# Convolution operand from a transposed input, row statistics on ScalarE, and the gate ahead of its neighbours

## The chip, the cores and the metric

The kernel runs on one core of one Trainium2 chip. The metric is the device time of one launch in microseconds, from the first instruction to the last. The engines are named as in the profile: PE is TensorE's matmul, PEld its weight load, DVE is VectorE, ACT is ScalarE, POOL is GpSimd, and SP is SyncE, which here issues nearly all DMAs as one queue.

## The reference, cut to what matters

The input x has 4 batches of 1024 rows of 2048 values. Each row is normalized and modulated, convolved along its 2048 values with a kernel K that comes from a state-space model, gated and added to x. Then each row is normalized and modulated again and goes through a 2048 by 2048 weight with a low-rank update, and is gated and added again.

```python
mod = (_silu(L0_c) @ L0_wmod).reshape(L0_c.shape[0], 6, 1, -1)
sa, ca, ga, sb, cb, gb = (mod[:, i] for i in range(6))
ga = (2 * (ga >= 0) - 1) * jnp.maximum(jnp.abs(ga), 0.25)    # gb likewise
h = _layernorm(x, axis=-1) * (1 + ca) + sa
K = _s4_kernel(...)                                          # 2048 taps
y = irfft(rfft(h, n=2*L) * rfft(K, n=2*L))[..., :L]          # causal convolution
x = x + ga * (y + D[0] * h)
h = _layernorm(x, axis=-1) * (1 + cb) + sb
x = x + gb * (h @ W.T + bias + low_rank_update(h))
```

All arithmetic of the matmuls is done in pairs of float16 numbers, a high and a low part, with three products for each.

## The kernel before, in words

**Tiles.** A "row" in this text is a block of 128 input rows, r = 0 to 31, so that a row tile is 128 x 2048 in float32 (1 MB). Eight rows are one batch. A chunk is 128 of the 2048 values, so that a row has 16 chunks.

**Modulation.** `section` multiplies the conditioning vector with one sixth of `wmod`: 16 loads `wm` of 1 MB (`mod_load`) and as many groups of four small matmuls `modps` (`mod_mm`, L317). A section becomes columns (`mod_column`: `sa`, `ca`, `sb`, `cb`) or a gate (`mod_gate`, L342 to L347). Sections 1, 0 and 2 are done first, since the convolution needs them; sections 4, 3 and 5 come later as filler.

**The convolution kernel.** `s4` works out K; its last steps are 32 tiny matmuls `s4rp` (L175) and `s4kp`. `toeplitz` writes K to DRAM and reads it back as a 128 x 2048 tile `kb` whose row p is shifted by p, so that slices of it are Toeplitz blocks. [...] a matmul with the reversed identity `rev` (L263) turns the rows round. Then `kb` is split into six float16 tiles `kh0`, `kl0` and so on, for the even blocks, the odd minus even, and the shifted difference (L281 to L285).

**One row.** `conv_load` fetches x. `stats` takes mean and variance with four `bn_stats` (L540) and `bn_aggr` on DVE, and `rstd` (L69 to L73) the inverse deviation. `conv_prep` makes the operand: `normalize` writes `n` on DVE (L557), then for each quarter (four chunks) PE transposes four 128 x 128 blocks into PSUM (`tp`, L578), ACT takes them out with scale and shift (`t`, L582; L587 for rows 0 and 1), DVE adds pairs of chunks (`sm`, L590), and ACT and DVE split `t` and `sm` into high and low parts (`hc`, `hs`, L592 and L593). `conv_mm` runs 108 matmuls (L614) in six families, `ya`, `yb`, `ya` for each half of the row; a copy `qs` on ACT (L627) and four or five DVE operations (L631 to L641) turn the sums into the new x, with its row sum. `conv_post` stores it in DRAM (`x1d`) and takes the second statistics with a squaring pass on ACT (L660), which writes its unused result over x.

**Early rows.** Rows 0 and 1 start before the shift `sa` and the gate are known (`EARLY = 2`). The shift's share is convolved by itself (`shift_conv`, L397) and added later (`shift_add`, L414), and the gate is applied in `conv_late`. `pace` places one `wm` step of sections 0 and 2 after every 2700 columns of convolution. For row 2, `behind` lets PE run `GCOL = 11000` columns ahead of the matmuls `gps` (L674), which spread the first gate over all partitions.

**Order.** The program text sets the order, row by row. Each row calls `tick` ten times, and `PLAN` says by letters what is put in at each call: `N` a quarter of the next operand, `T` the statistics of row r + 2, `F` the start of its operand, `P` the previous row's `conv_post`, `S` a step of the filler, `L` a step of the feed-forward's left operand in the last rows. The filler (`rest`) merges the low-rank update into the weight (`merge`: `lps`, `we`, `wch`, written to `wcd`) and does sections 4, 3 and 5. There are nine `S` per row from row 5 on, fewer before. The tile framework then places the instructions on the engines' queues and sets the waits.

```python
PLAN = ("PNSL", "NL", "NSL", "NTL", "SL", "SL", "SL", "SL", "FSL", "SSL")
WM, WMS = 3, 3
```

**Feed-forward.** After row 31, `ffn_unit` runs 5376 matmuls (L750) in seven products per unit. The left operand of later units (`left`, L700 to L713) is made beside it in its first half.

Of the kernel before, what the change touches and what calls it, by code (L numbers as in the profile page):

```python
# [34 lines left out]
class Net:  # L35
# [40 lines left out]
    def s4(self, pool):  # L76
# [69 lines left out]
        rp = self.tps.tile([P, 16, 8], F32, tag="t", name="s4rp")  # L146
# [19 lines left out]
        for n, (cc, sc) in enumerate(cps):  # L166
            tt(wq[n], wr[n], wq[n], ADD)
            v.reciprocal(wq[n], wq[n])
            stt(wr[n], cc, nl[:, 0:1], wq[n], MUL, MUL)
            tt(wi[n], wi[n], wq[n], MUL)  # L170
            yield
            for c in range(w // P):
                out = rp.rearrange("p (h g) v -> p g h v", h=2)[:, 4 * n + c]
                for i, x in enumerate((wr[n], wi[n])):
                    nc.tensor.matmul(  # L175
                        out, x[:, ds(P * c, P)], cf[:, i],
                        start=(n, c, i) == (0, 0, 0), stop=(n, c, i) == (1, 3, 1), skip_group_check=True,
                    )
        r = T([P, 8, 16], "s4R")
        v.tensor_copy(r.rearrange("p v k -> p k v"), rp)  # L180
# [51 lines left out]

    def toeplitz(self, pool):
        nc, v = self.nc, self.nc.vector
        rev = pool.tile([P, P], F32, tag="rev", name="rev")
        nc.gpsimd.memset(rev, 0.0)
        nc.gpsimd.affine_select(
            out=rev, in_=rev, compare_op=ALU.not_equal, fill=1.0, base=1 - P, pattern=[[1, P]], channel_multiplier=1
        )
# [15 lines left out]

        kb = pool.tile([P, D], F32, tag="kb", name="kb")
        src = bass.AP(tensor=kd.tensor, offset=kd.offset + 1, ap=[[1, P], [1, D]])
        nc.gpsimd.dma_start(out=kb, in_=src)
        self.kb = kb
        yield  # L260
        for q in range(4):
            ps = self.acc.tile([P, 512], F32, tag="a", name="kbps")
            nc.tensor.matmul(ps, rev, kb[:, ds(512 * q, 512)], start=True, stop=True)  # L263
            (v.tensor_copy if q % 2 else nc.scalar.copy)(kb[:, ds(512 * q, 512)], ps)
# [5 lines left out]
        for f in (0, 2, 1):  # L270
            hi = self.kpool.tile([P, HC * P], F16, tag=f"kh{f}", name=f"kh{f}")
            lo = self.kpool.tile([P, HC * P], F16, tag=f"kl{f}", name=f"kl{f}")
            h3, l3 = (x.rearrange("p (m t) -> p m t", t=P) for x in (hi, lo))
            if f == 0:
                src = ev
            else:
                src = pool.tile([P, 2, 512], F32, tag="kdif", name="kdif")
                src = src.rearrange("p a (c t) -> p (a c) t", t=P)
                if f == 1:
                    v.tensor_scalar(src[:, 0:1], ev[:, 0:1], -1.0, None, MUL)  # L280
                    v.tensor_tensor(src[:, 1:], od[:, 0 : HC - 1], ev[:, 1:], SUB)  # L281
                else:
                    v.tensor_tensor(src, od, ev, SUB)
            v.tensor_copy(h3, src)  # L284
            v.tensor_tensor(l3, src, h3, SUB)  # L285
            self.kf[f] = hi, lo
# [51 lines left out]
    def mod_gate(self, pool, name, bias=None):  # L338
# [8 lines left out]
        v.scalar_tensor_tensor(g, g, 1.0, m, SUB, MUL)  # L347
# [62 lines left out]
    def shift_add(self, pool, ys):  # L410
        g = pool.tile([P, D], F32, tag="gat", name="gsb")
        self.nc.gpsimd.dma_start(out=g, in_=self.gsd.rearrange("c t -> (c t)").partition_broadcast(P))
        for y in ys:
            self.nc.vector.tensor_tensor(y, y, g, ADD)  # L414
# [121 lines left out]
    def stats(self, pl, x, tag):  # L536
        v = self.nc.vector
        st = pl["sm"].tile([P, 4, 6], F32, tag="st" + tag, name="st" + tag)
        for q in range(4):
            v.bn_stats(st[:, q], x[:, ds(512 * q, 512)])  # L540
        mv = pl["sm"].tile([P, 2], F32, tag="mv" + tag, name="mv" + tag)
        v.bn_aggr(mv, st)
        rs = pl["sm"].tile([P, 1], F32, tag="rs" + tag, name="rs" + tag)
        self.rstd(pl["sm"], mv[:, 1:2], rs, 1, "r" + tag)
        if tag in ACTNORM:
            mb = pl["sm"].tile([P, 1], F32, tag="mb" + tag, name="mb" + tag)
            v.scalar_tensor_tensor(mb, mv[:, 0:1], -1.0, rs, MUL, MUL)
            return mb, rs
        return mv, rs

    def normalize(self, pl, x, st, tag):
        n = pl["n"].tile([P, D], F32, tag="n", name="n" + tag)
        m, rs = st
        if tag in ACTNORM:
            self.nc.scalar.activation(n, x, AF.Identity, bias=m, scale=rs)
        else:
            self.nc.vector.tensor_scalar(n, x, m[:, 0:1], rs, SUB, MUL)  # L557
        return n
# [6 lines left out]
    def conv_prep(self, pl, r, x, st, out, shift=True):  # L565
        nc, v = self.nc, self.nc.vector
        b = r // 8
        n = self.normalize(pl, x, st, "1")
        yield

        hc = [pl["h"].tile([P, NC, P], F16, tag=f"hc{x}", name=f"hc{x}") for x in range(2)]
        hs = [pl["h"].tile([P, HC, P], F16, tag=f"hs{x}", name=f"hs{x}") for x in range(2)]
        out[r] = hc, hs
        for c0 in range(0, NC, 4):
            tp = self.tps.tile([P, 4, P], F32, tag="t", name="tp")
            t = pl["t"].tile([P, 4, P], F32, tag="t", name="t")
            for k in range(4):
                nc.tensor.transpose(tp[:, k], n[:, ds(P * (c0 + k), P)], self.ident)  # L578
            for k in range(4):
                c = c0 + k  # L580
                if shift:
                    nc.scalar.activation(  # L582
                        t[:, k], tp[:, k], AF.Identity,
                        bias=self.sa[:, c, b : b + 1], scale=self.ca[:, c, b : b + 1],
                    )
                else:
                    nc.scalar.activation(t[:, k], tp[:, k], AF.Copy, scale=self.cae[:, c : c + 1])  # L587
            tv = t.rearrange("p (i e) n -> p i e n", e=2)
            sm = pl["t"].tile([P, 2, P], F32, tag="sm", name="sm")
            v.tensor_tensor(sm, tv[:, :, 0, :], tv[:, :, 1, :], ADD)  # L590
            for (hi, lo), src, sl in ((hc, t, slice(c0, c0 + 4)), (hs, sm, slice(c0 // 2, c0 // 2 + 2))):
                nc.scalar.copy(hi[:, sl], src)  # L592
                v.tensor_tensor(lo[:, sl], src, hi[:, sl], SUB)  # L593
            yield

    def conv_mm(self, pl, hs, x, tick, early, pace):
        nc, v = self.nc, self.nc.vector
        hc, hs = hs
        y = pl["y"].tile([P, D], F32, tag="y", name="y")
# [54 lines left out]
    def conv_post(self, pl, r, x, y, sums):  # L654
# [5 lines left out]
        nc.scalar.activation(x, y, AF.Square, bias=mn, accum_out=sq)  # L660
# [147 lines left out]
ACTNORM = ""  # L808

MR = 2  # L810
ACC, TPS = 5, 2
PLAN = ("PNSL", "NL", "NSL", "NTL", "SL", "SL", "SL", "SL", "FSL", "SSL")
LPLAN = ("LL", "LL", "LL", "LL", "L", "0", "")
R0 = 5
WM, WMS = 3, 3
ROWC = 2700
GCOL = 11000
# [15 lines left out]
def net(ctx: ExitStack, tc: tile.TileContext, io):  # L833
# [52 lines left out]
    for name, bufs in (("h", 2), ("n", 1), ("t", 2), ("y", EARLY), ("g", 1)):  # L886
        pl[name] = pool(left, "p1" + name, bufs)
# [25 lines left out]
    for _ in section(1, (wms, wmp)):  # L913
# [3 lines left out]
        if n == X0:  # L917
            load(0)
# [248 lines left out]
```

## Time and profile before

| | us |
|---|---|
| median of 3 runs | 2144.08 |
| lowest and highest run | 2141.26, 2145.41 |
| the profiled execution | 2141.87 |
| its span | 2140.1 |
| PE busy in it | 2082.4 (97%) |
| DVE busy | 1308.4 (61%) |
| ACT busy | 923.7 (43%) |
| first and last convolution matmul (L614) | 68.5 and 918.9 |
| first feed-forward matmul (L750) | 918.9 |

The page gives for each engine its busy time in the span. A group row of the page names a source line, the engine, what is written and read, and how many there were; then the busy time of the group, the mean duration of one, and the idle time of the engine just before them with what ended it. Recorded durations of neighbours on one engine may overlap, so that the busy time of a group is less than number times mean. A windows row gives, for a stretch of the span, the busy time of each engine with the number of instructions, then PE's granted clock, the mean share of the DMA engines and the rate. The DMA share is 0.98 in the first 60 us, and 0.57 in the feed-forward part.

### The profile page before, as it was taken

What the parts mean: (1) busy time and instruction counts of PE and PEld (TensorE: products, weight loads), DVE (VectorE), ACT (ScalarE), POOL (GpSimd) and SP (SyncE); (2) the same over time, 40 slices, a digit from 0 to 9 for tenths busy, and PEclk for the clock granted to TensorE, in tenths of its full rate; (3) what the DMA queues carried; (4) which work ended last, traced back from release to release, by engine and by line L of the source; (5) the groups of instructions that cost most, each with busy time, mean ns of one, the idle gap of its engine ahead of it and who ended that gap; (6) DMA issues with size and microseconds to landing.
All of it is one profiled execution on the core that took longest, in us unless ns stands there. A gap on an engine that the chain in (4) does not pass through costs nothing.

```text
span 2140.1 us, 28438 instructions
## 1 busy us (share of the span) xinstructions
PE 2082.4 (97%) x11113; PEld 1026.1 (48%) x11113; DVE 1308.4 (61%) x2353; ACT 923.7 (43%) x1695; POOL 6.3 (0%) x18
## 2 busy tenths in 40 slices
PE   7898999999999999999999999999999999999998
PEld 2344455555555555554545545555444444444444
DVE  5439898898979999665565565575533323332323
ACT  1325876677767777745454555555200000000000
POOL 0000000000000000000000000000000000000000
PEclk7999999999999999999999999999999999999999
DMA  9977566787776554387564564564794645454542
GB/s 401 373 307 278 225 227 265 285 310 262 276 278 227 187 192 173 139 346 258 190 241 180 202 240 179 203 235 172 283 341 163 192 151 167 164 170 165 177 157 69
DMA packets 127236, 484.11 MB, mean 226 GB/s; under 512 B 13608, under 2 KB 13768, under 8 KB 95998
## 3 DMA queue, kind: packets, MB, share of 16 engines
q1 hardware_dynamic: 126192, 477.55, 61.4%
q10 hardware_dynamic: 526, 2.63, 0.4%
q8 instruction: 87, 1.43, 0.3%
q0 software_dynamic: 384, 2.11, 0.2%
q14 instruction: 47, 0.39, 0.0%
HBM read 326.94 MB, written 155.30 MB: 225 GB/s over the span
## 4 chain that ended last, share of the span: by engine, by line
PE 67%; DVE 18%; ACT 6%; DMA 5%; issue 2%; SPq 0%; ACTq 0%; POOL 0%; DVEq 0%; POOLq 0%
PE fZ L750 22%; PE fY L750 15%; PE fX L750 15%; PE ya L614 5%; PE yb L614 3%; PE tp L700 3%; DVE wch L514 2%; PE modps L317 2%; DVE st L540 2%; DVE hc L593 2%; DVE y L641 2%; ACT x L660 2%; DMA wcd<-wch 1%; ACT t L582 1%; PE lps L486 1%
## 5 line engine op out<-in xcount | busy, mean ns | idle before, releaser
L750 PEld LDWEIGHTS <-lf 128*128 128x128 f16 x5376 | 526.0, 98 | 620.9 <-issue 1.4
L750 PE MATMUL fZ<-w,lf 128*128 128x512 f16 x2304 | 513.6, 379 | 0.8 <-ACT p L758 0.8
L750 PE MATMUL fX<-w,lf 128*128 128x512 f16 x1536 | 342.8, 379 | 0.0
L750 PE MATMUL fY<-w,lf 128*128 128x512 f16 x1536 | 342.0, 379 | 0.0
L614 PEld LDWEIGHTS <-hc 128*128 128x128 f16 x2304 | 215.3, 98 | 204.6 <-issue 41.6
L768 DVE TENSOR_TENSOR xo<-xo,gb 128x512 f32<-128x512 f32 x128 | 87.8, 690 | 238.7 <-DMA xo<-x1d 227.2
L582 ACT ACTIVATE t<-tp,sa,ca 128x128 f32<-128x128 f32 x480 | 188.1, 471 | 21.6 <-PE tp L578 12.9
L614 PE MATMUL ya<-kh,hs 128*128 128x512 f16 (+3 forms) x768 | 193.7, 326 | 3.7 <-DVE kh L284 2.6
L614 PE MATMUL ya<-kh,hc 128*128 128x512 f16 (+3 forms) x768 | 192.7, 328 | 3.8 <-ACT qs L627 3.6
L614 PE MATMUL yb<-kh,hc 128*128 128x512 f16 (+3 forms) x768 | 192.2, 327 | 1.8 <-DVE y L640 1.4
L758 ACT COPY p<-fZ 128x512 f32<-128x512 f32 x64 | 37.2, 581 | 286.8 <-PE fZ L750 272.1
L614 PEld LDWEIGHTS <-hs 128*128 128x128 f16 x1152 | 105.9, 98 | 108.6 <-issue 28.4
L758 ACT COPY p<-fX 128x512 f32<-128x512 f32 x32 | 18.7, 585 | 316.3 <-PE fX L750 210.4
L702 ACT ACTIVATE gt<-tp,sb,cb 128x256 f32<-128x256 f32 x256 | 124.9, 576 | 60.8 <-PE tp L700 60.8
L317 PE MATMUL modps<-wm,sct 128*32 128x512 f32 x768 | 118.8, 662 | 14.1 <-DMA wm<-in_wmod 14.1
L614 PE MATMUL ya<-kl,hc 128*128 128x512 f16 (+3 forms) x384 | 125.8, 328 | 0.0
L614 PE MATMUL ya<-kl,hs 128*128 128x512 f16 (+3 forms) x384 | 125.1, 326 | 0.7 <-DVE kl L285 0.7
L614 PE MATMUL yb<-kl,hc 128*128 128x512 f16 (+3 forms) x384 | 125.6, 327 | 0.0
L773 DVE TENSOR_TENSOR fin<-fX,gb 128x512 f32<-128x512 f32 x32 | 22.1, 692 | 128.4 <-PE fX L750 128.3
L593 DVE TENSOR_TENSOR hc<-t,hc 128x512 f16<-128x512 f32 x128 | 87.5, 684 | 6.6 <-ACT hc L592 6.4
L486 PE MATMUL lps<-lbh,lac 128*128 128x512 f16 x256 | 86.3, 379 | 1.2 <-DVE we L488 1.2
L578 PE MATMUL tp<-ident,n 128*128 128x128 f32 x512 | 79.3, 280 | 8.1 <-ACT t L582 6.3
(264 smaller groups left out, 2228.0 us busy)
## 6 DMA issues: line engine op xcount, KB each, us to landing
wm<-in_wmod SPq DMA_DIRECT2D x96, 1024.0 KB
lfd<-lf SPq DMA_DIRECT2D x112, 512.0 KB
lf<-lfd SPq DMA_DIRECT2D x112, 512.0 KB
x<-in_x SPq DMA_DIRECT2D x32, 1024.0 KB
x1d<-y SPq DMA_DIRECT2D x32, 1024.0 KB
x<-x1d SPq DMA_DIRECT2D x32, 1024.0 KB
xo<-x1d SPq DMA_DIRECT2D x128, 256.0 KB
out<-xo SPq DMA_DIRECT2D x128, 256.0 KB
```

The lines of the kernel that those rows point to most:

```text
L317: self.last = self.nc.tensor.matmul(self.modps[32 * g : 32 * g + 32, :], self.sct[:, j].rearrange("p r b -> p (r b)"), w[:, ds(512 * g, 512)],
L486: nc.tensor.matmul(ps, la[:, x, k, h], y[:, k, osl], start=(n == 0), stop=(n == 5))
L514: v.tensor_tensor(hl[:, :, 1, :], tv, hl[:, :, 0, :], SUB)
L578: nc.tensor.transpose(tp[:, k], n[:, ds(P * (c0 + k), P)], self.ident)
L582: nc.scalar.activation(t[:, k], tp[:, k], AF.Identity, bias=self.sa[:, c, b : b + 1], scale=self.ca[:, c, b : b + 1],)
L593: v.tensor_tensor(lo[:, sl], src, hi[:, sl], SUB)
L614: nc.tensor.matmul(pf[:, o:512], h, self.kf[f][z][:, ds(k0, 512 - o)], start=first, stop=(i == last and (x, z) == (1, 0)), skip_group_chec ...
L700: nc.tensor.transpose(tp[:, c, r], xs[r][:, ds(P * (c0 + c), P)], self.ident)
L702: nc.scalar.activation(t[:, c0 + c], tp[:, c], AF.Identity, bias=self.sb[:, c0 + c, b : b + 1], scale=self.cb[:, c0 + c, b : b + 1],)
L750: nc.tensor.matmul(ps[name], lf[i][:, k, x, :], wc[i][k // 4][:, k % 4, y, :], start=(first and n == 0), stop=(n == 3 * HC - 1), skip_grou ...
L758: nc.scalar.copy(t, ps[name])
L768: v.tensor_tensor(x, x, self.gbias[:, h], ADD)
```

## The change

It has five parts.

1. **The operand comes transposed.** The host lays x out a second time as `xT`, with the chunk's values on the partitions and the rows along the free dimension, for pairs of rows (a group g is rows 2g and 2g + 1). A quarter `xq` (four chunks of both rows, 0.5 MB) is loaded by `quarter_load`, five buffers in all. `quarter_norm` adds minus the mean and multiplies with the inverse deviation, which now vary along the free dimension, in two `tensor_tensor` passes over the quarter. `quarter_mod` applies scale and shift in place on ACT, for both rows at once. `split` makes `hc` and `hs`, with `hs` in halves instead of quarters. The 512 transposes `tp`, their evacuation and the tile `n` are gone.
2. **Statistics on ACT.** `stats` sums the row with one ACT pass, scales the sum on DVE, squares and sums in a second ACT pass, and takes `rstd`. The passes write to an unused tile `junk`. `spread` transposes the two 128 x 1 results, broadcast to 128 columns, with four PE transposes for each group into the PSUM tile `mrb`, where every partition then has all means and deviations. Statistics are made for row r + 3, and x is loaded for row r + 3. x is still loaded in the old layout, for the statistics and for the final sum.
3. **Opposite chunk rows.** In `xT`, and in the first two sections of `wmod`, the 128 values of a chunk stand in opposite order. The reversal of `kb` by matmul is gone; `kb` is loaded in two halves and split half by half. In `s4`, the 32 tiny matmuls become four of 16 x 512 and eight small transposes.
4. **Gate first.** The first gate tile and its `gps` matmuls come right after section 2 and before the other work of that place, and `shift_add` is held behind the gate's DVE chain (`issue_after(k.gated.ins)`). `GCOL` is 30000, and row 2 has its own tile `y2`, so that it needn't wait for those of rows 0 and 1.
5. **Plan and buffers.** `PLAN` differs for even and odd rows: `B` and `A` split a quarter for the next row, `X` loads a quarter, `K` spreads, `G` normalizes and modulates a quarter. There are eight `S` per row. `WM` is 2.

The diff, cut to its core:

```diff
+        sp = self.acc.tile([16, w], F32, tag="a", name="s4sp")
+        for i, x in enumerate((wr[n], wi[n])):
+            nc.tensor.matmul(sp, cf[:, i].rearrange("p h v -> p (h v)"), x, start=(i == 0), stop=(i == 1))
...
-        for q in range(4):
-            ps = self.acc.tile([P, 512], F32, tag="a", name="kbps")
-            nc.tensor.matmul(ps, rev, kb[:, ds(512 * q, 512)], start=True, stop=True)
-            (v.tensor_copy if q % 2 else nc.scalar.copy)(kb[:, ds(512 * q, 512)], ps)
...
+    def quarter_load(self, pl, g, q, blocks=(0, 1)):
+        t = pl["q"].tile([P, 2, 4, P], F32, tag="xq", name="xq")
+        b = slice(blocks[0], blocks[-1] + 1)
+        self.nc.sync.dma_start(out=t[:, b], in_=self.io["xT"][g, :, b, ds(4 * q, 4), :])
+        return t
+
+    def stats(self, pl, x):
+        nc, v = self.nc, self.nc.vector
+        st = pl["sm"].tile([P, 2], F32, tag="st", name="st")
+        nc.scalar.activation(self.junk, x, AF.Copy, accum_out=st[:, 0:1])
+        v.tensor_scalar(st[:, 0:1], st[:, 0:1], -1.0 / D, None, MUL)
+        sq = pl["sm"].tile([P, 1], F32, tag="sq1", name="sq1")
+        nc.scalar.activation(self.junk, x, AF.Square, bias=st[:, 0:1], accum_out=sq)
+        self.rstd(pl["sm"], sq, st[:, 1:2], 1, "r1", 1.0 / D)
+        return st
+
+    def spread(self, sts):
+        ps = self.tps.tile([P, 2, 2, P], F32, tag="t", name="mrb")
+        for b, st in enumerate(sts):
+            for i in range(2):
+                self.nc.tensor.transpose(ps[:, i, b], st[:, i : i + 1].to_broadcast([P, P]), self.ident)
+        return ps
+
+    def quarter_norm(self, t, ps, blocks=(0, 1)):
+        for i, op in enumerate((ADD, MUL)):
...
+            m = ps[:, i, b].unsqueeze(2).to_broadcast([P, n, 4, P])
+            self.nc.vector.tensor_tensor(t[:, b], t[:, b], m, op)
+
+    def quarter_mod(self, t, b, q, shift=True, blocks=(0, 1)):
...
+        for k in range(4):
+            c = 4 * q + k
+            x = t[:, bb, k]
...
+                self.nc.scalar.activation(
+                    x, x, AF.Identity, bias=self.sa[:, c, b : b + 1], scale=self.ca[:, c, b : b + 1]
+                )
+
+    def split(self, pl, h, t, q):
...
+        v.tensor_tensor(self.sm[:, ds(2 * (q % 2), 2)], tv[:, :, 0, :], tv[:, :, 1, :], ADD)
+        sl = slice(4 * q, 4 * q + 4)
+        nc.scalar.copy(hc[0][:, sl], t)
+        v.tensor_tensor(hc[1][:, sl], t, hc[0][:, sl], SUB)
+        if q % 2:
+            sl = slice(2 * q - 2, 2 * q + 2)
+            nc.scalar.copy(hs[0][:, sl], self.sm)
+            v.tensor_tensor(hs[1][:, sl], self.sm, hs[0][:, sl], SUB)
...
-PLAN = ("PNSL", "NL", "NSL", "NTL", "SL", "SL", "SL", "SL", "FSL", "SSL")
+PLAN = (
+    ("PBX", "BXL", "BXSL", "TSL", "BXSL", "SL", "KGSL", "SL", "GSL", "SL"),
+    ("PG", "GAL", "ASL", "TSL", "ASL", "SL", "ASL", "SL", "SL", "SL"),
+)
-WM, WMS = 3, 3
+WM, WMS = 2, 3
-GCOL = 11000
+GCOL = 30000
+QS = 5
...
+    k.gat = k.gate_tile(pl["g"], 0)
     take(nxt, 40)
-    k.shift_add(pl["g"], [ys[r][0] for r in range(2)])
+    with tc.issue_after(k.gated.ins):
+        k.shift_add(wms, [ys[r][0] for r in range(2)])
+    y2 = stp.tile([P, D], F32, tag="kb", name="y2")
```

## The prediction

> **What bounds the kernel now.** I read the page's busy line first, then the windows by stage, then the costliest groups, the waits and a piece of the timeline.
>
> ```profile
> PE 2082.4 (97%) x11113; PEld 1026.1 (48%) x11113; DVE 1308.4 (61%) x2353; ACT 923.7 (43%) x1695; POOL 6.3 (0%) x18
> ```
>
> TensorE (PE) is busy 97% of the whole span, but an average hides the stages. The windows (columns: window, length, busy us of PE, PEld, DVE, ACT, POOL, then granted clock, DMA share, GB/s) cut the span into start, the two early rows, the gate, rows 5 to about 25 with the weight merge beside them, the last rows, and the feed-forward part:
>
> ```profile
> 0.00:60.00 60.00, 41.47 (x185) 15.36 (x186) 34.01 (x127) 7.93 (x16) 3.92 (x13) 0.78 0.98 403
> 60.00:160.00 100.00, 93.84 (x583) 38.21 (x581) 40.17 (x83) 29.33 (x80) 1.51 (x3) 0.94 0.85 336
> 160.00:243.00 83.00, 69.97 (x400) 35.44 (x401) 72.97 (x168) 55.25 (x114) 0.51 (x1) 0.92 0.73 271
> 243.00:800.00 557.00, 545.95 (x3352) 288.35 (x3350) 503.48 (x1042) 396.63 (x802) 0.41 (x1) 1.00 0.67 248
> 800.00:919.00 119.00, 117.23 (x744) 68.93 (x742) 97.58 (x212) 85.63 (x181) 0.00 (x0) 1.00 0.47 173
> 919.00:2140.00 1221.00, 1213.94 (x5858) 579.80 (x5855) 560.24 (x727) 348.91 (x505) 0.00 (x0) 1.00 0.57 201
> ```
>
> From 243 on PE is busy 98% or more. From 243 to 919, 676 us, it holds 663.2 us of work; VectorE (DVE) holds 601.1 (89%) and ScalarE (ACT) 482.3 (71%). So PE bounds the convolution rows, and DVE follows only 62 us behind: that is the number to keep in mind. After 919 the change touches nothing.
>
> The groups that the change removes or resizes (busy us, mean ns of one):
>
> ```profile
> L578 PE MATMUL tp<-ident,n 128*128 128x128 f32 x512 | 79.3, 280 | 8.1 <-ACT t L582 6.3
> L582 ACT ACTIVATE t<-tp,sa,ca 128x128 f32<-128x128 f32 x480 | 188.1, 471 | 21.6 <-PE tp L578 12.9
> L540 DVE BATCH_NORM_STATS2 st<-x 128x6 f32<-128x512 f32 x128 | 84.0, 682 | 0.8 <-DMA x<-in_x 0.6
> L557 DVE TENSOR_SCALAR n<-x,mv,rs 128x2048 f32<-128x2048 f32 x32 | 42.9, 1340 | 0.1
> L593 DVE TENSOR_TENSOR hs<-sm,hs 128x256 f16<-128x256 f32 x128 | 53.4, 418 | 0.4 <-ACT hs L592 0.2
> L641 DVE SCALAR_TENSOR_TENSOR y<-y,x 128x1024 f32<-128x1024 f32 x60 | 73.0, 1216 | 0.5
> ```
>
> The PE timeline shows that transposes stand in the convolution's way. Here four take about half a us between two matmuls of one family:
>
> ```profile
> 807.71 0.38 PE L614 MATMUL yb<-kl,hc 128*128 128x512 f16 x1
> 808.15 0.65 PE L578 MATMUL tp<-ident,n 128*128 128x128 f32 x4
> 808.64 0.59 PE L614 MATMUL yb<-kh,hc 128*128 128x512 f16 x2
> ```
>
> The waits show the early losses, and what DVE pays for a sum that ACT forms:
>
> ```profile
> PE gps L674 <- DVE mg L347: 9.9, 1, 9.9
> DVE r_v L69 <- ACT x L660: 17.1, 12, 2.2
> ```
>
> **What the Trainium skill says.** "TensorE: Matmul & The Clock Gate", Part 4 (PE-mode transpose), gives about 275 ns for a transpose inside a kernel. The trace agrees on the duration (280) and corrects the price: overlapped, one occupies PE for 79.3/512 = 0.155 us. "Perfetto Trace Analysis", Identifying the Most-Contended Engine, warns that matmul busy time does not show how near PE is to its limit. In 243 to 919 the 2919 conv matmuls take 504.1 us, 0.173 each; a 512-column one starts every 0.216 us in the timeline and a row averages 384 columns, so 0.162 is their floor. The busy share is nearly real. "VectorE: DVE Perf Modes", The TRN2 errata, prices a float32 tensor_tensor at (N+151)/0.96 ns: 1224 for 1024 elements, and the tier table keeps it at one element per cycle, PSUM operand or not. The trace has 1216 to 1219 for 1024 elements, and 683 for 512 with PSUM (y<-ya,gat). "ScalarE: Activation LUTs", Rules for kernel authors, has about 0.3 us plus 0.83 ns per element, 0.51 for 256: an estimate, on the high side, since the 512-wide cast measures 0.640 where it gives 0.72.
>
> **The change, part by part, 243 to 919.** Here 26 rows are prepared (416 transposes); 24 rows get statistics.
>
> PE: 416 transposes go, 51.4 + 12.3 = 63.7 us in the windows of that tile. The spread adds 4 transposes for each pair of rows: 13 x 4 x 0.155 = 8.1. PE falls from 663.2 to 607.6.
>
> DVE: 96 bn_stats go (0.656 each, 63.0), 24 aggregates (0.26, 6.2), 26 normalizations (1.34, 34.8). In place of the last come 8 tensor_tensor of 1024 elements per pair, reading mean and scale from PSUM: 13 x 8 x 1.22 = 126.9. This is the dear part: one two-scalar pass becomes two full passes. The hs subtraction, 104 of 0.417, becomes 52 of 0.684: -7.8. One small scaling per row: 24 x 0.15 = 3.6. Sum +18.7: DVE rises from 601.1 to 620.
>
> ACT: 416 evacuations go (163.0). In comes the modulation from SBUF, 208 of 128x256, at 0.425 (cast of that size) to 0.51 (the page): 88 to 106; two passes over each row, 24 x 2 x (2.00 + 0.19) = 105; hs casts -11. Sum about +28: 510 us.
>
> So **DVE, at 620, passes PE at 608**. The merge steps are dealt out 8 per row instead of 9, so that they end two rows or so later and the load is more even. When DVE set the pace before (180 to 220), it was busy 39.3 of 40 us. But now it stands behind ACT twice a row for a sum, so I take 96.5%: 642 us, a gain of 34. At 98% it is 633 (gain 43), at 92% 674 (gain 2).
>
> DMA: x is now fetched twice, 1 MB more per row in 2 KB pieces. At 248 GB/s and a share of 0.67, full use is about 370 GB/s; 27 MB more cost some 73 us of that and lift the share to about 0.82. SP is one queue: load x(r+3) waits for the previous row's last DVE pass and the xq loads for the split that frees a buffer, with mod and merge transfers behind them. Mod loads have two buffers instead of three; PE did not wait for them after 243, so I cost that at nothing. If their lead is gone, a wait costs up to the 7.9 us of the worst one in the start.
>
> **Before 243.** The reversal matmuls (5.4 us) go and kb comes in two halves. But DVE now has k's splitting (8.3 us by its rows) and eight norm passes (9.8) in line before row 0: from kb at about 55, plus 2.9 for the first splits, the first conv matmul comes at about 76, not 68.5. Eight quarters of xT, 4.2 MB at 400 GB/s, add 10 us of transfers ahead of the gate. Against that, 96 transposes (15.6 us) leave PE. At the gate, the 7 us of shift, statistics and normalization ahead of it on DVE step behind, and PE may run 30000 columns of row 2 instead of 11000 before it needs the gate: 19000 x 0.42 ns = 8 us of cover for the 9.9 us wait. DVE then has its backlog (early rows, 20 us), so row 4 starts about 8 us sooner. I take -8, bounds -20 and +8. The small s4 transposes replace tiny matmuls on an equal chain: nothing, within 1 us.
>
> Sum: profiled execution 2141.9 (span 2140.1), minus 34, minus 8 = 2100. The median shown is 2.2 above the profiled one: **2102**.
>
> **Rivals.** *PE stays the bound* (norm passes overlap better than I price them): 607.6 at the old 98.1% is 619, gain 57; with 15 early, 2072. For it: neighbouring DVE starts lie 0.60 apart where the record says 0.68. Against it: DVE would have to run at 99% or more.
>
> *ACT's sums become DVE's wait, and the kernel is slower.* The place is the pair L552 and L69 of the changed kernel: DVE scales the sum, ACT squares the row (2.2 us), DVE resumes. One or two DVE instructions stand between in the changed order, and at times none. Everything behind it in DVE's line, evacuation of y included, stands too, and PE at the spread. Before, the same handshake once a row cost 17.1 us over 32 rows; now there are two, and ACT is fuller. DVE at 97% is 639; it decides from (676 + 8 - 639)/26 = 1.7 us per row. At 2.5 us: 639 + 65 = 704, minus 8 early, 20 more than now: 2164.
>
> *The start eats it*: row 0 later by 15 rather than 7.5 and a stage at 94% (gain 16): about 2128.
>
> That the change doesn't do what it says is excluded for the transposes: its instruction order has 64 spread transposes instead of 512.
>
> **How the numbers follow.** DVE bound, near 2102 (2085 to 2120): 0.55. PE bound: 0.15. Start or utilization poor, 2120 to 2140: 0.14. No change, within 0.2% (4.3 us, about what a measurement can tell): 0.04. Slower: 0.12. So faster 0.84. The range 2068 to 2142 leaves about 0.05 below and 0.14 above.
>
> **What would show it.** Right: no tp group; transposes of mrb at about 10 us; norm passes at 1.2 us; in the conv rows DVE above 95% and PE below it; rows of about 25 us with merge (26.6 now); the feed-forward part at 1221 us. Wrong: DVE idle before L69 for more than 1.7 us per row, PE at 98%, or waits for xq or wm.

## The result, and the profile after

The changed kernel takes **2178.5 us** (median of 4 runs, 2171.4 to 2179.3) against 2143.5 for the kernel before on the same chip: a ratio of 1.0156, 95% interval 1.0133 to 1.018. The forecast was 2102, a gain of some 42 us, with 0.12 on slower. The prediction is wrong: the kernel is 35 us slower.

The profiled execution (2178.8 us, span 2177.0) splits as follows. "Row n's store" is the time at which SP issues the store of that row's result, read from SP's timeline. Here and below, the times of stages are those of one profiled execution of each kernel; the ratios of the experiments are to the kernel before on the same chip.

| | before | after | difference | forecast |
|---|---|---|---|---|
| row 0's store | 181.8 | 197.0 | +15.2 | |
| row 0's to row 4's store | 64.7 | 78.4 | +13.7 | both together: -8 |
| row 4's to row 31's store | 676.4 | 684.0 | +7.6 | -34 |
| last store to the end | 1217.2 | 1217.6 | +0.4 | 0 |

"The rows" below is the third line. Seven kernels that change only what lies before it, the changed kernel among them, gave 679.1 to 691.7, so differences under some 8 us there are not read as effects; the 7.6 themselves say no more than that the 34 did not come.

First the page's busy line after, which is no alarm in itself: PE went from 97% to 94%.

```profile
PE 2045.0 (94%) x10641; PEld 976.3 (45%) x10641; DVE 1324.4 (61%) x2263; ACT 990.5 (45%) x1503; POOL 6.4 (0%) x17
```

Then the windows after, by the same stages (length, busy us of PE, PEld, DVE, ACT, POOL, granted clock, DMA share, GB/s):

```profile
60.00:160.00 100.00, 76.37 (x435) 30.01 (x436) 47.70 (x100) 39.67 (x74) 1.30 (x3) 0.80 0.81 324
160.00:275.40 115.40, 94.76 (x532) 43.72 (x530) 72.58 (x149) 62.98 (x100) 0.98 (x2) 0.88 0.75 274
275.40:959.40 684.00, 629.78 (x3683) 317.62 (x3681) 615.63 (x1176) 525.78 (x811) 0.41 (x1) 0.98 0.75 270
959.40:2177.00 1217.60, 1211.41 (x5847) 578.91 (x5845) 556.90 (x723) 348.40 (x504) 0.00 (x0) 1.00 0.57 202
```

The third line is the heart of it. VectorE has 615.6 us of work in the rows, 4 from the 620 forecast, but it is busy 90.0% of the time, not 96.5%. PE is still the busiest, with 629.8 us or 92.1%; it is idle for 54 us and runs at a granted clock of 0.98. No engine is full. The same stretch of the kernel before (the last store comes at 922.9), where PE is idle for about 13:

```profile
246.50:923.00 676.50, 663.67 (x4085) 356.55 (x4084) 602.72 (x1252) 479.26 (x981) 0.41 (x1) 1.00 0.64 236
```

The groups of the rows, shapes kept apart (columns as before):

```profile
L571 DVE TENSOR_TENSOR xq<-xq,mrb 128x1024 f32<-128x1024 f32 x99 | 119.5, 1212 | 2.2 <-PE mrb L563 2.2
...
L579 ACT ACTIVATE xq<-xq,sa,ca 128x256 f32<-128x256 f32 x200 | 103.9, 588 | 28.3 <-DVE xq L571 28.3
...
L554 ACT ACTIVATE junk<-x,st 128x2048 bf16<-128x2048 f32 x24 | 48.0, 1999 | 4.3 <-DVE st L552 4.3
L551 ACT ACTIVATE junk<-x 128x2048 bf16<-128x2048 f32 x24 | 45.7, 1906 | 20.2 <-DMA x<-in_x 20.2
...
L563 PE MATMUL mrb<-ident,st 128*128 128x128 f32 x48 | 10.4, 289 | 6.9 <-DVE st L552 5.0 <-DVE st L73 1.8
```

The norm passes cost what was forecast (1.21). The modulation on ScalarE has a recorded duration of 0.588 each, but neighbouring records overlap: 200 of them keep ScalarE busy for 103.9 us, 0.52 each, at the upper end of the forecast's 0.425 to 0.51.

What PE waits for in the rows is scattered (columns: us in total, times, longest):

```profile
PE ya L625 <- DVE we L487: 9.4, 2, 6.8
PE ya L625 <- ACT qs L638: 8.9, 10, 3.2
PE mrb L563 <- DVE st L552: 5.0, 3, 1.9
PE lps L485 <- DVE y L651: 4.1, 2, 3.7
PE yb L625 <- DVE y L642: 4.0, 1, 4.0
```

Added up over all rows of this view, PE waits 53.8 us: 34.0 are ended by VectorE, 16.2 by ScalarE and 3.6 by a DMA. In the kernel before it is 12.0 (3.3, 8.7 and 0). Most of the places shown are evacuations of PSUM. Two moments show why they come late. On VectorE's timeline the sum y (L642), whose PSUM tile PE needs back, stands behind merge and norm passes of 1.2 us each; there is no gap between them:

```profile
802.93 1.22 DVE L513 TENSOR_TENSOR wch<-we,wch 128x1024 f16<-128x1024 f32 x1
804.07 1.22 DVE L571 TENSOR_TENSOR xq<-xq,mrb 128x1024 f32<-128x1024 f32 x1
805.20 1.22 DVE L530 TENSOR_TENSOR we<-we 128x1024 f32<-128x1024 f32 x1
806.34 0.21 DVE L669 TENSOR_SCALAR mn<-sums 128x1 f32<-128x1 f32 x1
806.46 1.21 DVE L571 TENSOR_TENSOR xq<-xq,mrb 128x1024 f32<-128x1024 f32 x1
807.59 0.68 DVE L642 TENSOR_TENSOR y<-yb,qs 128x512 f32<-128x512 f32 x1
```

PE's timeline at the same place and 17 us earlier (the bracket is the idle time before, and its releaser):

```profile
791.48 0.38 PE L625 MATMUL ya<-kh,hc 128*128 128x512 f16 x1 [3.16 <-ACT qs L638]
...
808.33 0.38 PE L625 MATMUL yb<-kh,hc 128*128 128x512 f16 x1 [3.96 <-DVE y L642]
```

The wait at 791 is ScalarE's version: the copy qs starts at 790.87, straight after a 2.0 us pass for the statistics.

### The profile page after: what moved, and what is told of

Read it like the earlier page. It is cut to its first block, busy times and chain, and to the rows that moved or that the text cites. A ratio compares the mean times of both kernels' runs of the same rounds, so it can differ in the third digit from the quotient of the medians.

```text
span 2177.0 us, 27282 instructions
## 1 busy us (share of the span) xinstructions
PE 2045.0 (94%) x10641; PEld 976.3 (45%) x10641; DVE 1324.4 (61%) x2263; ACT 990.5 (45%) x1503; POOL 6.4 (0%) x17
## 4 chain that ended last, share of the span: by engine, by line
PE 61%; issue 27%; DVE 5%; DMA 3%; ACT 3%; POOL 0%; SPq 0%; POOLq 0%; ACTq 0%; DVEq 0%
PE fZ L761 23%; PE fX L761 15%; PE fY L761 15%; PE ya L625 3%; PE tp L711 3%; DMA wm<-in_wmod 2%; PE modps L316 1%; PE yb L625 1%; DVE xq L571 1%; ACT xq L579 1%; DMA laf<-in_A 0%; DMA kb<-kd 0%; ACT hc L594 0%; DVE wch L513 0%; ACT xq L583 0%
## 5 line engine op out<-in xcount | busy, mean ns | idle before, releaser
L625 PEld LDWEIGHTS <-hc 128*128 128x128 f16 x2304 | 216.6, 99 | 232.7 <-issue 74.4
L625 PE MATMUL ya<-kh,hs 128*128 128x512 f16 (+3 forms) x768 | 201.3, 338 | 41.6 <-ACT hs L598 23.7
L571 DVE TENSOR_TENSOR xq<-xq,mrb 128x1024 f32<-128x1024 f32 x128 | 154.2, 1213 | 8.1 <-PE mrb L563 8.0
L579 ACT ACTIVATE xq<-xq,sa,ca 128x256 f32<-128x256 f32 x240 | 124.8, 588 | 31.8 <-DVE xq L571 31.8
L625 PE MATMUL ya<-kl,hs 128*128 128x512 f16 (+3 forms) x384 | 130.0, 338 | 0.0
L595 DVE TENSOR_TENSOR hc<-xq,hc 128x512 f16<-128x512 f32 x128 | 86.6, 682 | 13.1 <-ACT hc L594 12.9
```

Of the source, the lines that this page charges most:

```text
L571: self.nc.vector.tensor_tensor(t[:, b], t[:, b], m, op)
L579: self.nc.scalar.activation(x, x, AF.Identity, bias=self.sa[:, c, b : b + 1], scale=self.ca[:, c, b : b + 1])
L595: v.tensor_tensor(hc[1][:, sl], t, hc[0][:, sl], SUB)
L625: nc.tensor.matmul(pf[:, o:512], h, self.kf[f][z][:, ds(k0, 512 - o)], start=first, stop=(i == last and (x, z) == (1, 0)), skip_group_chec ...
```

## Experiments in the rows

**POOL's queue for the loads of xq.**

```diff
-        self.nc.sync.dma_start(out=t[:, b], in_=self.io["xT"]...)
+        self.nc.gpsimd.dma_start(out=t[:, b], in_=self.io["xT"]...)
```

> The changed kernel, with the loads of the transposed input issued on POOL's queue instead of SP's, so that nothing stands behind a load that waits for a free buffer. In the changed kernel row 4's store comes at 275.4 us (246.5 before) and the rows from there to the last store take 684.0 us (676.4 before). Theory Q (SP's queue: a load that waits for its buffer holds up the modulation weights and the merge's transfers behind it): row 4's store at 255 to 262, the rows 665 to 675, in all 2145 to 2158. Theory H (VectorE stands behind ScalarE's sums twice a row): row 4's store perhaps some us earlier, the rows within 5 us of 684, in all 2168 to 2178. Theory V (VectorE's work, 614 us in the rows, is the limit by its amount): the rows 684 as well; only the start could move.

Measured: 2189.6, ratio to before 1.0225 (1.0196 to 1.0255). Row 0's store 194.9, row 4's 273.1, the rows 698.5. Theory Q's gain did not come: with the loads on POOL the rows are 14.5 us longer, and in the changed kernel PE waits only 3.6 us of the rows for a DMA. So nothing here says that SP's queue holds up the rows. The start moved little, but this run does not clear SP there: kb is loaded on POOL's queue too, the copy of the first section came at 69.7 instead of 62.9, and the first convolution matmul at 84.3 instead of 77.5.

**No statistics on ScalarE**, from row 6 on.

```diff
-        sts[r] = k.stats(pl, xs[r])
+        sts[r] = k.stats(pl, xs[r]) if r < 6 else st6
```

> The changed kernel without ScalarE's two passes for the statistics from row 6 on: all these rows take row 5's statistics (that part of the computation is left out). It takes 26 x 4.4 = 114 us from ScalarE and both handshakes of a row from VectorE, and adds nothing. Theory H (handshake): VectorE's waits for the sums, some 21 us, and what hangs on them go; the rows fall from 684 to 650-660. Theory Q (SP's queue) and theory V (amount of VectorE work; it loses only 6 us): the rows stay at 675 to 682. If ScalarE's own load is what PE waits for (the casts of qs and hs stand behind the passes), the rows fall as under H, but with PE's waits for qs and hs (9.2 and 4) gone and VectorE's others unchanged. Row 4's store stays at 275.

**Statistics on VectorE**, from row 6 on.

```diff
-        sts[r] = k.stats(pl, xs[r])
+        sts[r] = k.stats(pl, xs[r]) if r < 6 else k.stats_dve(pl, xs[r])
```

> The changed kernel with the statistics of the rows from 6 on formed by VectorE (bn_stats) as in the kernel before: VectorE +26 x 2.9 - 6 = +69 us, ScalarE -114 us, no handshake. Theory V (VectorE's amount limits): the rows go from 684 to about 735-750. Theory H: the handshake's 21 us come back, so they go to about 710-725. Theory Q: VectorE at 683 us of work then is full anyway, 700 to 715. Row 4's store stays at 275.

**One norm pass**, from row 6 on.

```diff
-        k.quarter_norm(quarters[g][q], mr[g])
+        k.quarter_norm(quarters[g][q], mr[g], ops=(ADD, MUL) if g < 3 else (ADD,))
```

> The changed kernel with one norm pass instead of two from row 6 on: the mean is subtracted, the multiplication by the scale is left out. VectorE loses 13 x 4 x 1.21 = 63 us. Theory V: the rows fall by 40 to 60, to 625-645, until PE (628 busy) bounds them. Theory H: the waits stay, the rows fall by 10 to 25, to 660-675. Theory Q: by less than 10. Row 4's store stays at 275.

Measured: without statistics the rows take 654.1 (-29.9; 2139.8 in all, ratio 0.9987, 0.997 to 1.0004); with statistics on VectorE 698.5 (+14.5; 2186.7); with one norm pass 658.4 (-25.6; 2150.8). The windows of the rows, in this order:

```profile
265.60:919.70 654.10, 622.42 (x3698) 315.99 (x3698) 597.61 (x1053) 431.02 (x692) 0.52 (x1) 0.98 0.80 286
```

```profile
269.00:967.50 698.50, 640.21 (x3701) 319.76 (x3699) 664.74 (x1296) 433.00 (x713) 0.52 (x1) 0.97 0.75 268
```

```profile
273.20:931.60 658.40, 621.27 (x3688) 315.70 (x3685) 562.82 (x1121) 524.51 (x812) 0.41 (x1) 0.98 0.78 281
```

No theory (Q: SP's queue, H: VectorE's waits for the sums, V: VectorE's amount of work) gets all three. Two comparisons change VectorE's work alone. One norm pass less takes 53 us from VectorE, with ScalarE as it was, and brings 26. And the first two kernels have the same ScalarE (431 and 433) and neither waits for ScalarE's sums of x, but the second has 67 us more on VectorE; its rows are 44 us longer. So a us of VectorE's work is worth about a half to two thirds of itself (a third to three quarters with the scatter of 8 us): it counts, but it is not the whole bound.

What ScalarE's passes cost is not separated. Leaving them out takes 95 us from ScalarE, but also 18 us of small operations from VectorE (6 were expected) and VectorE's 21.5 us of waits for the sums. PE's waits in that kernel fall from 53.8 to 31.2 us; those that VectorE ends fall from 34.0 to 7.6, those that ScalarE ends only from 16.2 to 11.2. The wait for qs, which was to go if ScalarE's passes held it up, is still there (8.9 in the changed kernel):

```profile
PE ya L625 <- ACT qs L638: 10.1, 13, 1.6
```

**Late sums**: the same ScalarE passes, no handshake between them.

```diff
-        v.tensor_scalar(st[:, 0:1], st[:, 0:1], -1.0 / D, None, MUL)
-        nc.scalar.activation(self.junk, x, AF.Square, bias=st[:, 0:1], accum_out=sq)
-        self.rstd(...)
+        nc.scalar.activation(self.junk, x, AF.Square, accum_out=st[:, 1:2])
...
-        mr[g] = k.spread([sts.pop(2 * g + i) for i in range(2)])
+        mr[g] = k.spread([k.stats_end(pl, sts.pop(2 * g + i)) for i in range(2)])
```

> The changed kernel with the same two passes of ScalarE over each row, but independent of each other (sum, and sum of squares without the mean as bias; the variance is formed from both), and all of VectorE's small operations on them moved from the statistics step to the spread, three ticks later and for two rows together. ScalarE's work stays (within 1 us), VectorE gets some 32 x 0.3 = 10 us of small operations more. So far: leaving ScalarE's passes out took 29.9 us from the rows (684.0 to 654.1). If that was the wait of VectorE for the sums (theory H), this kernel gets most of it: the rows at 658 to 668, VectorE's waits for the sums under 8 us instead of 21, in all 2152 to 2164. If it was ScalarE's load (the casts of qs and hs that PE waits for stand behind 114 us of passes; theory A), the rows stay at 680 to 690 and PE's waits for qs and hs stay at 13.

Measured: 2172.2 (ratio 1.0154, 1.0137 to 1.0171), the rows 680.1. VectorE's waits for the two sums fell from 21.5 to 9.7 us, with 8 us more work, and the rows did not move beyond the scatter. Theory H's 658 to 668 did not come. PE's waits for qs and hs stayed at 12.9, as theory A has it, but A's other sign, that they go with the passes, had failed. And VectorE's work and waits together shrank here by only 4 us, so the run cannot tell what a us of such waiting costs. Neither theory is shown.

**The sums on POOL**: additions of 64 columns in place of ScalarE's first pass.

```diff
-        nc.scalar.activation(self.junk, x, AF.Copy, accum_out=st[:, 0:1])
+        for i in range(2, 32):
+            g.tensor_tensor(t, t, x[:, ds(64 * i, 64)], ADD)
...
```

> The changed kernel with ScalarE's first pass over each row (the plain sum) replaced by additions on POOL, which is idle (34 small ones a row, then a last reduction of 8 elements by VectorE); the squares stay on ScalarE, and the small operations stand at the spread as in the kernel with late sums. ScalarE loses 27 x 2.1 = 57 us in the rows, VectorE gains about 10. The late sums alone took 3.9 us from the rows (684.0 to 680.1). Theory A (ScalarE's load: qs and hs, which PE waits for, stand behind the passes): half of what leaving both passes out brought, so the rows at 665 to 672, in all 2157 to 2166. Rival D (VectorE's queue alone: a PSUM evacuation behind four or five passes of 1.22 us): the rows at 678 to 688. Rival P (POOL is slower than 26 us a row or hinders VectorE): 690 and more.

Measured: 2407.2 (ratio 1.1239, 1.1214 to 1.1264). An addition of 64 columns took 433 ns on POOL, so the 34 additions of a row take some 14 us, and VectorE stands for the sum:

```profile
DVE st L565 <- POOL psum L558: 163.1, 22, 11.3
```

The rows take 855.7. Rival P; the run decides nothing between A and D.

**Less PE work, nothing else changed**, in the kernel before and in the changed one.

```diff
-                    for x, z in ((0, 0), (0, 1), (1, 0)):
+                    for x, z in ((0, 0), (0, 1), (1, 0))[: 2 if f == 1 and self.less and i < last else 3]:
```

> The kernel before with 10 of the 108 matmuls of each row from row 6 on left out (the product of the low half of the data with the high half of the kernel, in the third family, all but the last of each half): 4352 columns a row, about 1.8 us a row, 47 us in all, from PE alone. VectorE and ScalarE keep all their work. If PE bounds the rows as the prediction has it, they fall from 676 to 630-640 (VectorE has 601). If the rows are held by the other engines' queues as much as by PE, they fall by 10 to 25, to 651-666. If PE's busy time is mostly waiting, by less than 8.

> The changed kernel with the same 10 matmuls a row left out. PE falls from 630 to about 583 us in rows that take 684. If PE no longer bounds at all: within 6 us of 684. If it still shares in the bound (PE waits, then works off what came late): 660 to 676. If PE alone bounds, 637 to 645. Row 4's store stays at 275.

The windows of the rows, of the kernel before and of the changed kernel, each with this edit:

```profile
241.30:882.20 640.90, 622.52 (x3827) 331.98 (x3826) 598.43 (x1251) 477.19 (x982) 0.41 (x1) 1.00 0.67 249
```

```profile
276.60:947.80 671.20, 595.62 (x3435) 296.62 (x3434) 612.21 (x1176) 523.14 (x811) 0.42 (x1) 0.95 0.76 275
```

Measured: 2102.3 (ratio 0.9833, 0.981 to 0.9857) and 2166.4 (1.0133). In the kernel before the rows fall by 35.5 us for 41 us less of busy PE; in the changed kernel by 12.8 for 34. So PE did bound the rows before, and taking PE work away while adding none elsewhere gained nearly all of it there. VectorE is then busy 93.4% of the rows, so in the order of the kernel before a share near the forecast's was within reach. In the changed kernel only a third of the PE time taken away is gained: PE waits for the others (74.6 us, 51.9 of them ended by VectorE), and its granted clock is 0.95.

**Neither statistics nor second pass**, from row 6 on: both edits above together.

> The changed kernel from row 6 on without ScalarE's statistics (row 5's are used) and without the multiplication by the scale (both are left out of the computation). If the two are separate causes, the rows fall by 29.9 + 25.5 = 55 to about 629, where PE (some 608 at full clock) is the bound again, and the total is 2110 to 2122. If either removal frees the same slack, the rows end at 645 to 655 and the total at 2130 to 2140.

```profile
260.50:909.60 649.10, 619.97 (x3712) 315.55 (x3711) 549.34 (x1007) 431.90 (x696) 0.41 (x1) 0.99 0.81 288
```

Measured: 2129.5 (ratio 0.9947, 0.9928 to 0.9967), the rows 649.1, -34.9 where the sum would be -55.5. The two removals free largely the same slack: with either alone PE is already busy 95% or 94% of the rows, and with both 95.5%. Even so relieved, the rows end at 649, not at the 619 of the rival "PE stays the bound".

## Experiments in the start

SP's timeline of the changed kernel shows the first suspect:

```profile
57.65 0.55 SPq L544 DMA_DIRECT2D xq<-in_xT  x1
59.03 0.33 SPq L311 DMA_DIRECT2D wm<-in_wmod  x1
83.80 0.55 SPq L544 DMA_DIRECT2D xq<-in_xT  x1
```

The second quarter of rows 2 and 3 needs the buffer that row 1's split of the first quarter frees, which happens beside row 0's matmuls. SP issues nothing for 24 us, with the modulation weights behind this load.

**k's splitting behind the first statistics.**

```diff
-    with tc.issue_after(k.last.ins):
+    with tc.issue_after(k.last.ins), tc.issue_after(rst.ins):
         take(toe, 1)
```

> The changed kernel with VectorE's splitting of the convolution kernel (which waits for kb until 53.6 us) put behind the small operations of the first two rows' statistics, which it stood in front of. Theory S (statistics stand behind kb on VectorE, so ScalarE stands too and the copy of the first modulation section comes at 62.9 instead of about 58): copy at 57 to 58, first convolution matmul at 70 to 73 instead of 77.5, row 0's store at 190 to 193 instead of 197.0, row 4's at 268 to 271 instead of 275.4, in all about 2171. Rival (the second section's weights set the gate, and they hang on SP's queue and on the 4 MB more that are fetched): first matmul earlier, but row 0's store within 2 us of 197.

Measured: 2171.5 (1.0154, 1.0125 to 1.0184). The first section's copy came at 56.9 as expected, the first convolution matmul at 75.8, but row 0's store only at 196.2. The rival holds.

**Rows 2 and 3's quarters loaded behind row 0's matmuls.**

```diff
     def second():
         for q in range(4):
             split(1, q)
-            qload(1, q)
             yield
     def third():
+        for q in range(4):
+            qload(1, q)
```

> The changed kernel with the loads of rows 2 and 3's transposed quarters moved from row 0's matmuls (where the second of them waits on SP from 59.4 to 83.8 us for a buffer, with modulation weights behind it) to the start of row 1's. Theory G (SP's blocked queue delays the gate): DMA share in 60 to 80 us from 0.63 to over 0.85, second section's copy at 115 to 119 instead of 125.4, row 0's store at 187 to 191 instead of 197.0, in all 2166 to 2172. Rival (PE takes no weights in that time anyway: its buffers stay full until the copy of the first section and the first convolution): row 0's store at 194 to 198, as with the loads on POOL's queue (194.9).

Windows from 80 to 100 us, of the changed kernel and of this one:

```profile
80.00:100.00 20.00, 12.12 (x69) 3.81 (x69) 8.31 (x19) 9.66 (x16) 0.00 (x0) 0.76 0.73 270
```

```profile
80.00:100.00 20.00, 20.00 (x135) 6.46 (x133) 6.21 (x16) 7.78 (x12) 0.00 (x0) 0.99 0.85 338
```

Measured: 2167.8 (1.0137, 1.0117 to 1.0157). Row 0's store at 180.9: **16.1 us back**, all of the loss up to there (10.7 of it in the total; the rows came at 686.5, within their scatter). PE's waits for modulation weights in the first 205 us fall from 33.8 to 14.7 us (13.4 before the change), and the second section's copy comes at 109.3 instead of 125.4. Theory G, and more than it expected.

**Statistics of rows 4 and 5 from an early copy**, first as they come, then (with the two edits above) behind the gate's operations.

```diff
+    for r in (4, 5):
+        with tc.issue_after(k.lastw.ins):
+            xt = wms.tile([P, D], F32, tag="wm", name="xt")
+            nc.sync.dma_start(out=xt, in_=io["x"][ds(P * r, P), :])
+        sts[r] = k.stats(pl, xt)
...
-    stats(4)
```

> The changed kernel with the statistics of rows 4 and 5 formed from a first copy of these rows, fetched behind the last modulation weight of the gate into buffers that are then free, instead of after rows 0 and 1 have left their buffers (at 197 to 208). 2 MB more are fetched. Theory R (row 4's operand is formed for rows 4 and 5 together and waits for row 5, which waits for row 1's buffer): the gap from row 0's store to row 4's falls from 78.4 to 66-70 (64.7 in the kernel before), row 4's store at 263 to 267, in all 2166 to 2170. Rival (that stretch is ScalarE's and VectorE's work on rows 0 to 5, whatever its order): the gap stays at 75 to 79.

> The changed kernel with three moves in the start together: rows 2 and 3's transposed quarters loaded after row 0's matmuls (alone: row 0's store at 180.9 instead of 197.0), the splitting of k behind the first statistics (alone: -0.8 at that store), and rows 4 and 5's statistics from an early copy, but this time behind the gate's own operations, where ScalarE otherwise stands from 168.9 to 182.2 us. If the loss from row 0's store to row 4's (78.4 us against 64.7) is ScalarE's four passes and the pair that waits for row 5, row 4's store comes at 246 to 251 and the total at 2150 to 2157. If it is the amount of work of VectorE and ScalarE there, row 4's store comes at 256 to 260 and the total at 2160 to 2166.

Measured: 2183.3 (1.021) with row 0's store at 201.4 and a gap of 72.7 to row 4's; then 2165.1 (1.0107) with row 0's store at 180.7 and a gap of 74.4. In the first the gap shrinks by what the gate loses; the second gains 4 us in the gap. Waiting for row 5 explains a part of it at most. PE's longest wait in the gap of the changed kernel is 11.3 us at 234.75, for hs from ScalarE; in the second of these kernels the longest for hs is 5.0, and in the kernel before no wait of PE in the gap is longer than 1.1.

**All of the start and the sums on POOL.** The sums on POOL and the three moves of the start in one kernel:

```diff
+            g.tensor_tensor(t, t, x[:, ds(64 * i, 64)], ADD)
...
+        for q in range(4):
+            qload(1, q)
...
+            xt.append(wms.tile([P, D], F32, tag="wm", name="xt"))
...
```

> The moves in the start and the sums on POOL in one kernel. If the effects add (start: -16 to -27, rows: -12 to -19 under theory A), 2132 to 2150, around the time of the kernel before. Under rival D of the rows 2150 to 2160.

Measured: 2397.3 (1.1195); POOL's sums decide it, as they did alone.

**The gate part alone, on the kernel before.**

```diff
+    k.gat = k.gate_tile(pl["g"], 0)
-    k.shift_add(pl["g"], [ys[r][0] for r in range(2)])
-    st.close()
+    with tc.issue_after(k.gated.ins):
+        k.shift_add(wms, [ys[r][0] for r in range(2)])
...
-GCOL = 11000
+GCOL = 30000
...
-    with tc.issue_after(k.lastw.ins):
-        next(fill)
```

> The kernel before with the gate part of the change alone: gate tile built ahead of the rest, the addition of the shift behind the gate's chain, row 2 allowed 30000 columns ahead of the gate matmuls instead of 11000, and buffers of the start kept until row 3. The prediction gave this part a gain of some 7 + 8 us of cover for the 9.9 us wait. If that holds, row 4's store comes at 237 to 240 instead of 246.5 and the total is 2131 to 2136. If what stands behind the gate (early rows, 20 us of VectorE, then row 4's operand) is the limit, not the wait, 2138 to 2146.

Measured: 2149.8 (ratio 1.0034, 1.0023 to 1.0046), slower by some 7 us. PE's wait for the gate did go (0.6 us instead of 9.9), but row 0's store did not move (181.7 against 181.8). Row 4's store came at 262.0, 15.5 later, and the rows took 665.4, 11 less. ScalarE's timeline of this kernel shows a likely cause of part of the 15.5:

```profile
240.15 3.89 ACT L445 ACTIVATE lb<-lb,lwt 128x2048 f32<-128x2048 f32 x2 [11.44 <-DMA lb<-in_BfT]
```

The start's buffers are kept until row 3's step, so the buffers of the low-rank preparation open later. Its load lb is issued at 226.2 instead of 199.7, and ScalarE stands 11.4 us for it, in front of a cast hs for which PE then waits (3.2 us). In the same stretch PE waits 9.8 us for modulation weights (0.7 before), so this run does not say how the 15.5 divide. (In the changed kernel lb is issued at 238.6, but ScalarE does not wait for it.)

**The gate part undone in the changed kernel**, alone and with the later loads: the reverse of that diff.

> The changed kernel with the gate part undone: shift first, then the gate tile, 11000 columns of row 2 ahead of the gate matmuls, the start's buffers freed before row 2 and the merge's preparation begun behind the gate's last modulation weight, as before. The gate part alone cost the kernel before 15.5 us at row 4's store and gave 11 back in the rows. If it does the same here: the gap from row 0's store to row 4's falls from 78.4 to 63-66, the rows rise to 690-695, in all 2170 to 2175. If row 4's operand (pair of rows, ScalarE's statistics) sets the gap here, it stays at 74 to 80.

> The changed kernel with the gate part undone and the loads of rows 2 and 3's quarters moved behind row 0's matmuls. If both add: row 0's store at 181 to 184, row 4's at 246 to 250, in all 2150 to 2160. If only the loads count: 2163 to 2168.

Measured: 2167.9 (1.014; gap from row 0's store to row 4's 74.9, the rows 679.1) and 2158.8 (1.0093, 1.0072 to 1.0113; row 0's store 185.3, gap 75.1). The gate part costs the changed kernel 3 to 4 us of the gap, and the two repairs do not quite add. Of the 13.7 us that the gap grew, this part accounts for those 3 to 4; the statistics of rows 6 and 7, which fall into it, account for some 7 (the kernel without statistics from row 6 on has a gap of 71.1). The rest is not settled. No complete kernel of these beats the kernel before.

## Why the prediction was wrong, point by point

- **"PE bounds the convolution rows"**: right. Taking PE time alone from the kernel before brought 35.5 us.
- **The sums of work**: VectorE 620 forecast, 615.6 measured; ScalarE 510 against 525.8; PE 607.6 against 629.8, so that VectorE did not pass PE. On ScalarE the groups' busy times, added one by one, grew by 27 us, as forecast (28). But the engine's busy time grew by 46.5: neighbouring records overlap, by 63 us in all before and by 43 after, and the forecast took the busy time of whole groups off a busy time in which they overlap others. On PE the clock of 0.98 is worth some 12 of the 22 (an estimate: 2% of 608); the rest is not broken down.
- **"so I take 96.5%"**: the failed step of the rows. The measured share is 90.0%, and 615.6/0.90 gives the 684. The 96.5% came from the 98% of a stretch of 40 us (180 to 220) in which "DVE set the pace"; but PE was busy 38.8 of these 40 us too, and only ScalarE had room (28.2). One short stretch is no measure for 26 rows in another order. Here PE, VectorE and ScalarE are at 92, 90 and 77%, and VectorE and ScalarE hold, behind their long passes, small operations that another engine needs: y and qs for PE, the sums for VectorE. PE waits 53.8 us instead of 12. The prediction's own lower end, 92% for a gain of 2 us, was the nearer one.
- **The rival "ACT's sums become DVE's wait, and the kernel is slower"**: its sign came true, its price did not. VectorE waits 11.2 us at L69 and 10.3 at L552, 0.8 per row where 1.7 was to decide. The statistics do cost 30 us in the rows, but how much of it is this wait, VectorE's small operations or ScalarE's passes stays open.
- **"I take -8, bounds -20 and +8"**: the failed step of the start; measured +28.9. It priced the first matmul rightly (76; it came at 77.5) and the gate's cover rightly (the 9.9 us wait went), but neither sets the end there. It did say that on SP the xq loads wait "for the split that frees a buffer, with mod and merge transfers behind them", and gave this no price in the start, where it cost 16. Of the 13.7 after row 0's store, the statistics of rows 6 and 7 and the gate part account for some 11 as measured above; the prediction gave neither a cost there.
- **"I cost that at nothing"** (mod loads with two buffers): right in the rows, where PE waits 3.6 us for wm. In the start the waits rose by 20, nearly all of it SP's stop.
- **Unchanged feed-forward part, norm passes at 1.2, spread at about 10 us**: right (1217.6 and 1217.2; 1.21; 10.4). The DMA share is 0.75, not 0.82: in time it grew by 80 us where 73 were forecast, but the forecast started from the 0.67 of 243 to 800, where all of the rows had 0.64, and spread it over shorter rows.

## What to carry to other kernels

Relieving a full engine is worth its time only while the engines that take over have room in their order, not just in their sum: with two at about 90% and a third near 80%, a us of VectorE's work was worth here about a half to two thirds of itself, and a us of PE's a third. A share of busy time from a short stretch is no forecast for a new order of work, and a group's busy time is not what its removal takes from its engine. Follow every load that waits for a buffer on the queue it shares, and name what stands behind it; one such load cost 16 us, and moving four loads by one row gave it back. When buffers are kept longer, ask which later stage was to be built in their place, and look when its loads are issued.

## What the runs showed of the hardware that was not expected

- PE's granted clock sank where PE had little to do: in the changed kernel to 0.59 in the window from 60 to 80 us with PE busy 8.0 of 20 (0.98 and 16.7 in the kernel before), and in the rows to 0.95 when PE work was taken away from the changed kernel. The runs show the two together, not which causes which.
- An addition of 128x64 in float32 took 433 ns on POOL, and one of 128x8 took 215: half of the time for an eighth of the columns (the run with the sums on POOL).
